# The second layer's context in one run of matmuls instead of two halves, with its pointwise work moved to other slots

## The chip, the cores and the metric

The kernel runs on one core of one Trainium2 chip. The metric is the time on the device in microseconds (us), the median of several executions. Engines are named as the profile names them: PE is TensorE, DVE is VectorE, ACT is ScalarE, POOL is GpSimd, SP is SyncE with the DMA queue.

## The reference, cut to what matters

128 samples of 64 tokens with 768 features go through a two-layer graph attention, all in float32, and `x` is added at the end:

```python
h = jnp.maximum(_layernorm(x, axis=-1), 0.0)
for l in range(2):
    ...                                   # attention from h, W_left, W_right, adj
    h_lin = jnp.einsum('bsh,oh->bso', h, W_lin[l]) + b_lin[l]
    ctx = jnp.matmul(attention, h_lin)    # 64x64 by 64x768 for each sample
    h = relu(_layer_norm(ctx, ln_a[l], ln_b[l]))
return x + h
```

The last pass of the kernel computes the last three lines of layer 1, for 16 blocks (0 to 15) of 8 samples. A block is four tiles of 128 tokens by 768.

## The kernel before

TensorE forms `h_lin` of a block from 15 products (0 to 14) of sums of token columns with sums of weights. Each product goes to one of the PSUM banks X, Y, Z, V, and ScalarE or VectorE adds the bank into `hl`. Two products that use the same bank wait for each other: product 10 writes the bank X that product 8 has left, so it needs VectorE's two reads of product 8. GpSimd forms the 11 token sums `ts` of the next block from `ht`, after ScalarE has applied the affine (`Relu(scale * ht + bias)`) to it.

The context of block `u - 1` is computed between the products of block `u`. In the second layer it comes in two halves, behind products 0 and 7, and its pointwise work is put at numbered slots, two a product (slot 2i after the first half of product i, slot 2i+1 after its read). A slot sets only the place in each engine's queue.

```python
def scaled(k):                                     # in finish(u, r): one half
    if last:
        nc.vector.scalar_tensor_tensor(zs[k], cx[k], rs[:, k:k + 1], rows["a"], op0=ALU.mult, op1=ALU.mult)
        nc.gpsimd.tensor_add(zs[k], zs[k], rows["b"])          # the bias sum
        return
    ...
def done(k):
    if last:
        xs = XS[u, r]                              # the residual sum: max with 0, plus x
        nc.vector.scalar_tensor_tensor(xs[k], zs[k], 0.0, xs[k], op0=ALU.max, op1=ALU.add)
        ...                                        # store, then load the next x
...
put_all(9 if u else 15, affine(2, l, u + 1))             # ScalarE: one of six a slot
put_sums_t((2, l, u + 1), 15 if u else 21, 1, 0)         # GpSimd: the 11 sums
ends = {}
if u and last:
    ends = {0: ((u - 1, 0), (6, 7, 8, 11, 12)), 7: ((u - 1, 1), (20, 21, 22, 30, 30))}
elif u > NB - 3:
    ends = {5: ((u - 1, 0), (16, 17, 18)), 11: ((u - 1, 1), (28, 29, 30))}
elif u:
    ends = {12: (u - 1, None)}                     # layer 0: the whole context behind product 12
```

The five slot numbers of a half are those of the inverse deviation, two scalings and two residual sums. (Reshapes are cut from the code.)

Of the kernel before, what the change touches and what calls it, by code (L numbers as in the profile page):

```python
# [10 lines left out]
F32 = mybir.dt.float32  # L11
I32 = mybir.dt.int32
AF = mybir.ActivationFunctionType
ALU = mybir.AluOpType
# [3 lines left out]
def kernel(  # L18
# [24 lines left out]
    nc = tc.nc  # L43
    B, S, H = x.shape
# [32 lines left out]
    def put(slot, *fs):  # L77
        plan.setdefault(slot, []).extend(fs)

    def put_all(slot, fs, step=1):  # L80
        for f in fs:
            if f is not None:
                put(slot, f)
            slot += step
        return slot
# [537 lines left out]
    def pass_two(l, aside):  # L623
        last = l == L - 1
        with tc.tile_pool(name=f"two{l}", bufs=2, reuse_waits="tile") as sp:
# [48 lines left out]
            def batch(r, k, h):  # L674
                return 4 * (h if k == 0 else 1 - h) + r + 2 * k
# [46 lines left out]
            def residual(u, r):  # L722
                XS[u, r] = [sp.tile([P, H], F32, name="xr", bufs=4) for _ in range(2)]
                for k in range(2):
                    for h in range(PAIR):
                        nc.sync.dma_start(XS[u, r][k][h * S:(h + 1) * S], x[u * NBB + batch(r, k, h)])  # L726

            def finish_block(u, more):

                parts = context_block(u)  # L730
                tiles = ((0, 0), (0, 1), (1, 0), (1, 1))
                zs = {t: sp.tile([P, H], F32, name="z", bufs=4) for t in tiles}
                cut = (slice(0, T), slice(T, H))

                for t in ((1, 1), (1, 0)):
                    nc.vector.tensor_copy(zs[t][:, cut[0]], parts[t][0])
                    parts[t][0] = zs[t][:, cut[0]]
                    if t == (1, 1):
                        AHEAD.append(fresh(l, 0, more))
                ss = stat.tile([P, Q, 2], F32, name="ssb", bufs=2)  # L740
                sd = stat.tile([P, Q], F32, name="sdb", bufs=2)
                rs = stat.tile([P, Q], F32, name="rsb", bufs=2)

                def squares(t):
                    junk = zs[0, t[1]]
                    for n in range(2):
                        nc.scalar.activation(junk[:, cut[n]], parts[t][n], AF.Square,
                                             accum_out=ss[:, 2 * t[0] + t[1], n:n + 1])

                def deviation():  # L750
                    nc.vector.reduce_sum(sd, ss, axis=mybir.AxisListType.X)
                    nc.scalar.activation(sd, sd, AF.Sqrt, bias=floor, scale=1.0 / (H - 1.0))

                def inverse():
                    nc.vector.tensor_scalar_add(rs, sd, EPS_LN)
                    nc.vector.reciprocal(rs, rs)

                def scaled(t):
                    by = rs[:, 2 * t[0] + t[1]:2 * t[0] + t[1] + 1]
                    for n in range(2):  # L760
                        nc.scalar.activation(zs[t][:, cut[n]], parts[t][n], AF.Copy, scale=by)
                    kept(u, *t, zs[t])

                order = ((1, 1), (1, 0), (0, 0), (0, 1))
                for f, slots in ((squares, (25, 26, 28, 29)), (scaled, (33, 34, 35, 36))):
                    for n, t in zip(slots, order):
                        put(n, lambda f=f, t=t: f(t))
                put(30, deviation)
                put(32, inverse)

            def kept(u, r, k, z):
                for h in range(PAIR):
                    nc.sync.dma_start(ROWS[u][batch(r, k, h)], z[h * S:(h + 1) * S])

            def finish(u, r):

                cx = context(u, r)
                zs = [sp.tile([P, H], F32, name="z", bufs=4) for _ in range(2)]
                if last and not u and not r:
                    residual(u, r)  # L780
                two = "p (n d) -> p n d"
                ss = stat.tile([P, 2], F32, name="ss", bufs=2)
                sd = stat.tile([P, 2], F32, name="sd1", bufs=2)
                rs = stat.tile([P, 2], F32, name="rs1", bufs=2)
                for k in range(2):
                    nc.scalar.activation(zs[k].rearrange(two, n=2), cx[k], AF.Square, accum_out=ss[:, k:k + 1])

                nc.scalar.activation(sd, ss, AF.Sqrt, bias=floor, scale=1.0 / (H - 1.0))

                def inverse():  # L790
                    nc.vector.tensor_scalar_add(rs, sd, EPS_LN)
                    nc.vector.reciprocal(rs, rs)

                def scaled(k):
                    if last:
                        nc.vector.scalar_tensor_tensor(  # L796
                            zs[k].rearrange(two, n=2), cx[k], rs[:, k:k + 1],
                            rows["a"].rearrange(two, n=2), op0=ALU.mult, op1=ALU.mult)
                        nc.gpsimd.tensor_add(zs[k], zs[k], rows["b"])  # L799
                        return  # L800
                    if (u, r, k) == (NB - 1, 1, 1):
                        nc.vector.tensor_scalar_mul(zs[k].rearrange(two, n=2), cx[k], rs[:, k:k + 1])
                    else:
                        nc.scalar.activation(zs[k].rearrange(two, n=2), cx[k], AF.Copy, scale=rs[:, k:k + 1])
                    kept(u, r, k, zs[k])

                def done(k):
                    if last:
                        xs = XS[u, r]
                        nc.vector.scalar_tensor_tensor(xs[k], zs[k], 0.0, xs[k], op0=ALU.max, op1=ALU.add)  # L810
                        for h in range(PAIR):
                            nc.sync.dma_start(out[u * NBB + batch(r, k, h)], xs[k][h * S:(h + 1) * S])
                        if k and u + r < NB - 1:
                            residual(u + r, 1 - r)

                steps = [lambda f=f, k=k: f(k) for f in (scaled, done) for k in range(2)]
                return [inverse] + (steps if last else steps[:2])

# [36 lines left out]
            for u in range(NB):  # L855
                turn = not last and u >= NB - 2
                put(4, lambda u=u: load_at(u))
                if u + 1 < NB:
                    load_h(2, l, u + 1)
                    put_all(9 if u else 15, affine(2, l, u + 1))  # L860
                    put_sums_t((2, l, u + 1), 15 if u else 21, 1, 0)
                    if turn:
                        load_rows(1, 0, sp)
                        put_all(10, transpose_rows(1, 0, sp), 2)
                    if u in aside:
                        aside[u]()
                    ends = {}
                    if u and last:
                        ends = {0: ((u - 1, 0), (6, 7, 8, 11, 12)), 7: ((u - 1, 1), (20, 21, 22, 30, 30))}
                    elif u > NB - 3:  # L870
                        ends = {5: ((u - 1, 0), (16, 17, 18)), 11: ((u - 1, 1), (28, 29, 30))}
                    elif u:
                        ends = {12: (u - 1, None)}
                    linear(u, (0, 1), 0, ends, (0, 1) if u + 2 < NB else (0,))
                    for n in sorted(plan):
                        plan[n - 30] = plan.pop(n)
                else:
                    if turn:
                        load_h(1, 1, 0)
                        put_all(28, affine(1, 1, 0), 3)  # L880
                        put_sums_t((1, 1, 0), 38, 2, 30)
                        ends = ({1: ((u - 1, 0), (13, 14, 16)), 11: ((u - 1, 1), (34, 35, 36))},
                                {4: ((u, 0), (50, 51, 52))})
                    else:
                        last_block(u)
                        ends = ({0: ((u - 1, 0), (12, 13, 15, 22, 24)), 9: ((u - 1, 1), (28, 29, 30, 39, 41))},
                                {2: ((u, 0), (44, 48, 51, 61, 62))})
                    linear(u, (0,), 0, ends[0], (1,))
                    linear(u, (1,), 30, ends[1], ())
                    for n in sorted(plan):  # L890
                        run(n)
                    for f in (finish_last if last else finish)(u, 1):
                        f()
# [48 lines left out]
```

## Time and profile before

| | us |
|---|---|
| time, median of 3 | 2758.04 (2754.77 to 2759.26) |
| span of the profiled run | 2756.7 |
| TensorE busy | 2726.2 |
| one steady block of the last pass | 29.20 |
| one block of the first layer, context in one run | 28.84 |

The view of busy time by stretch, for one steady block of the last pass. The columns are the stretch and its length, then the busy time of PE, PEld, DVE, ACT and POOL with their instruction counts, then the granted TensorE clock (1.00 is full speed), the DMA share and GB/s.

```profile
core 0: us, PE busy (x) PEld busy (x) DVE busy (x) ACT busy (x) POOL busy (x), PEclk, DMA share, GB/s
2392.16:2421.36 29.20, 29.20 (x156) 23.59 (x152) 19.89 (x25) 13.63 (x26) 23.64 (x16) 1.00 0.59 167
```

TensorE has not a gap in 29.20 us. VectorE (19.89) and GpSimd (23.64) both have idle time, but a residual sum of VectorE can't be placed anywhere in it: the 60 of the last pass (128x768) take 946 ns at best and 2023 in the median, and two took 4.00 us at 2401.78, while GpSimd worked throughout.

### The profile page before, as it was taken

Reading aid. Unit: us, or ns where it says so; the run is one execution under the profiler, and the core shown is the slowest. Engines: PE = TensorE matmul, PEld = TensorE weight load, DVE = VectorE, ACT = ScalarE, POOL = GpSimd, SP = SyncE. Lnnn points to the kernel's source line nnn. Section 1 sums busy time; section 2 is a strip of 40 time slices with the busy share of each in tenths; the row PEclk is TensorE's granted clock in tenths of the full one; section 3 lists DMA queues with packets and bytes.
Section 4 is the critical chain, followed back from the end, with each engine's and each line's share of the span. In section 5 each row is a group of like instructions: output and inputs, shape, how many; then the busy total and the mean of one; then the engine's idle time right before and its main releaser. Section 6 shows DMA issues by size and latency. Waiting matters only on the chain. (4 is left out here: it accounts for less than half of the span.)

```text
span 2756.7 us, 46373 instructions
## 1 busy us (share of the span) xinstructions
PE 2726.2 (99%) x18712; PEld 2339.2 (85%) x18712; DVE 1347.4 (49%) x2269; ACT 849.5 (31%) x1611; POOL 1192.3 (43%) x935
## 2 busy tenths in 40 slices
PE   8999999999999999999999999999999999999998
PEld 7888888888888888888788888888888887888886
DVE  6455445545454333333335444544444335676666
ACT  3222223222321154444621211121122214444443
POOL 3432352224223555655522443223222325887885
PEclk9999999999999999999999999999999999999999
DMA  6534433343332333343555333443344204555655
GB/s 196 128 75 98 121 81 81 90 120 90 76 80 72 102 109 117 116 155 124 149 126 151 94 75 78 116 112 75 76 101 120 57 26 145 164 168 164 178 161 143
DMA packets 234072, 310.82 MB, mean 113 GB/s; under 512 B 54146, under 2 KB 184450, under 8 KB 225666
## 3 DMA queue, kind: packets, MB, share of 16 engines
q1 hardware_dynamic: 233698, 307.45, 41.6%
q8 instruction: 149, 2.44, 0.4%
q14 instruction: 65, 0.53, 0.1%
q10 hardware_dynamic: 160, 0.39, 0.0%
HBM read 202.91 MB, written 104.86 MB: 112 GB/s over the span
## 5 line engine op out<-in xcount | busy, mean ns | idle before, releaser
L155 POOL TENSOR_TENSOR ts<-ht 128x512 f32<-128x512 f32 x441 | 586.7, 1340 | 1223.8 <-DMA ht<-h 523.1
L203 ACT ACTIVATE m<-X 128x512 f32<-128x512 f32 (+1 forms) x256 | 151.5, 592 | 1086.0 <-PE X L429 570.1
L155 POOL TENSOR_TENSOR ts<-ht,ts 128x512 f32<-128x512 f32 x189 | 248.8, 1323 | 135.4 <-PE X L833 60.6
L155 DVE TENSOR_TENSOR m<-m,V 128x512 f32<-128x512 f32 (+1 forms) x256 | 173.3, 677 | 270.0 <-PE V L429 269.8
L155 DVE TENSOR_TENSOR m<-m,X 128x512 f32<-128x512 f32 (+1 forms) x256 | 162.9, 677 | 249.8 <-PE X L429 249.1
L833 PE MATMUL X<-w_n,ts 128*128 128x256 f32 x1024 | 244.3, 380 | 2.5 <-ACT X L619 1.7
L429 PE MATMUL X<-ts,w_l 128*128 128x256 f32 x1024 | 242.7, 380 | 0.1
L429 PE MATMUL X<-ts,w_r 128*128 128x252 f32 (+1 forms) x1024 | 238.7, 376 | 0.0
L155 DVE TENSOR_TENSOR m<-m,Z 128x512 f32<-128x512 f32 (+1 forms) x128 | 87.5, 683 | 306.0 <-ACT m L203 246.1
L833 PEld LDWEIGHTS X<-w_n,ts 128*128 128x128 f32 x1024 | 191.5, 190 | 35.0 <-issue 3.1
L429 PEld LDWEIGHTS X<-ts,w_l 128*128 128x128 f32 x1024 | 192.0, 190 | 30.2 <-DVE m L155 2.7
L429 PEld LDWEIGHTS X<-ts,w_r 128*128 128x128 f32 x1024 | 192.0, 190 | 26.0
L275 ACT ACTIVATE ht<-ht,b_col,a_col 128x512 f32<-128x512 f32 x192 | 143.6, 804 | 151.3 <-DMA ht<-h 151.3
L833 PE MATMUL Y<-w_n,ts 128*128 128x256 f32 x768 | 182.5, 379 | 0.0
L429 PE MATMUL Y<-ts,w_l 128*128 128x256 f32 x768 | 181.5, 379 | 0.4 <-DVE w_l L155 0.4
L429 PE MATMUL Y<-ts,w_r 128*128 128x252 f32 (+1 forms) x768 | 179.2, 376 | 1.3 <-POOL w_r L155 1.3
L429 PEld LDWEIGHTS Y<-ts,w_l 128*128 128x128 f32 x768 | 145.8, 190 | 20.6 <-DVE w_l L155 0.8
L833 PEld LDWEIGHTS Y<-w_n,ts 128*128 128x128 f32 x768 | 145.8, 190 | 20.4 <-issue 0.6
L429 PEld LDWEIGHTS Y<-ts,w_r 128*128 128x128 f32 x768 | 145.8, 190 | 19.1 <-POOL w_r L155 1.7
L155 DVE TENSOR_TENSOR hl<-hl,V 128x512 f32<-128x512 f32 (+1 forms) x136 | 89.0, 655 | 129.4 <-PE V L833 112.1
L203 ACT ACTIVATE hl<-X 128x512 f32<-128x512 f32 (+1 forms) x135 | 77.9, 577 | 222.2 <-PE X L833 219.3
L799 POOL TENSOR_TENSOR z<-z,b 128x768 f32<-128x768 f32 x62 | 111.9, 1816 | 79.4 <-DVE z L796 79.4
(163 smaller groups left out, 4729.5 us busy)
## 6 DMA issues: line engine op xcount, KB each, us to landing
ht<-h SPq DMA_DIRECT2D x63, 1536.0 KB, 7.2
h<-xb SPq DMA_DIRECT2D x124, 384.0 KB, 5.9
z<-z SPq DMA_DIRECT2D x128, 192.0 KB, 3.1
x<-z SPq DMA_DIRECT2D x128, 192.0 KB, 8.5
x<-in_x_dram SPq DMA_DIRECT2D x120, 192.0 KB, 8.4
xr<-in_x_dram SPq DMA_DIRECT2D x120, 192.0 KB, 3.8
out_dram<-xr SPq DMA_DIRECT2D x120, 192.0 KB, 2.7
adj<-in_adj_dram SPq DMA_DIRECT2D x64, 128.0 KB, 2.7
```

The source lines that it names most:

```text
L155: (eng.tensor_add if sign == "+" else eng.tensor_sub)(o, a, b)
L203: nc.scalar.activation(to(o), p, AF.Copy, scale=1.0 if sign == "+" else -1.0)
L275: nc.scalar.activation(ht, ht, AF.Relu, bias=cols[1][:, c:c + 1], scale=cols[0][:, c:c + 1])
L429: nc.tensor.matmul(p[:, g], w[ORDER[i][0]][:, c, g * P:(g + 1) * P], b()[t][:, c, :].rearrange(bs, s=S)[:, :, :ns], start=(new and g == c ...
L799: nc.gpsimd.tensor_add(zs[k], zs[k], rows["b"])
L833: nc.tensor.matmul(p[:, n], b[t][:, c, r * P:(r + 1) * P], w[s][:, c, :], start=(i in FIRST and i not in PRELOAD and n == c == 0), stop=(c ...
```

## The change

Its intent: the last pass does as the first layer does, so that TensorE changes between its 128x128 and its 64x64 tiling once a block instead of twice. In blocks 1 to 10 the context of the block before stands in one run behind product 12; the four residual sums stand in a row behind the read of product 5, "where GpSimd rests". The last five blocks step back to halves, each a little earlier, since the end needs them early. In block 12 the affines and GpSimd's sums stand four slots later (`late`).

```diff
 def finish_block(u, more):                # the whole context of a block
-        nc.vector.tensor_copy(zs[t][:, cut[0]], parts[t][0])
+        (nc.scalar.copy if last else nc.vector.tensor_copy)(zs[t][:, cut[0]], parts[t][0])
 ...
+                        if last:
+                            nc.vector.scalar_tensor_tensor(to, parts[t][n], by, rows["a"][:, cut[n]],
+                                                           op0=ALU.mult, op1=ALU.mult)
 ...
+                    if last:
+                        nc.gpsimd.tensor_add(zs[t], zs[t], rows["b"])
 ...
+                put_each(squares, (26, 27, 28, 29) if last else (25, 26, 28, 29))
+                put_each(scaled, (29, 30, 33, 34) if last else (33, 34, 35, 36))
+                if last:
+                    put_each(lambda t: added_to(u, *t, zs[t]), (41, 42, 43, 44))   # slots 11 to 14 of the next block
 ...
-                    put_all(9 if u else 15, affine(2, l, u + 1))
-                    put_sums_t((2, l, u + 1), 15 if u else 21, 1, 0)
+                    late = 4 if last and u == NB - 4 else 0
+                    put_all(late + (9 if u else 15), affine(2, l, u + 1))
+                    put_sums_t((2, l, u + 1), late + (15 if u else 21), 1, 0)
 ...
-                    if u and last:
-                        ends = {0: ((u - 1, 0), (6, 7, 8, 11, 12)), 7: ((u - 1, 1), (20, 21, 22, 30, 30))}
+                    ends = {12: (u - 1, None)} if u else {}
+                    if last and u > NB - 6:       # blocks 11, 12, 13, 14; NB is 16
+                        ends = ({8: ((u - 1, 0), (22, 23, 24, 31, 33)), 13: ((u - 1, 1), (32, 33, 34, 39, 41))},
+                                {5: ((u - 1, 0), (16, 17, 18, 30, 32)), 11: ((u - 1, 1), (28, 29, 30, 36, 38))},
+                                {3: ((u - 1, 0), (12, 13, 14, 15, 16)), 9: ((u - 1, 1), (24, 25, 26, 32, 33))},
+                                {1: ((u - 1, 0), (8, 9, 10, 13, 14)), 7: ((u - 1, 1), (20, 21, 22, 30, 30))})[u - NB + 5]
+                    if last and u:
+                        residuals(u - 1, ...)     # loads of x at slots of their own
```

Left out: the split of the deviation into two pairs of tiles, and the same rearrangement in block 15.

More of the change, by code (lines that the diff above doesn't have):

```diff
@@ L726, in residual, with residuals @@
                         nc.sync.dma_start(XS[u, r][k][h * S:(h + 1) * S], x[u * NBB + batch(r, k, h)])
+            def residuals(u, slots):
+                for r, slot in sorted(enumerate(slots), key=lambda s: s[1]):
+                    put(slot, lambda r=r: residual(u, r))
             def finish_block(u, more):
                 parts = context_block(u)
-                tiles = ((0, 0), (0, 1), (1, 0), (1, 1))
-                zs = {t: sp.tile([P, H], F32, name="z", bufs=4) for t in tiles}
+                order = ((1, 1), (1, 0), (0, 0), (0, 1))
+                zs = {t: sp.tile([P, H], F32, name="z", bufs=4) for t in order}
                 cut = (slice(0, T), slice(T, H))
-                for t in ((1, 1), (1, 0)):
-                    nc.vector.tensor_copy(zs[t][:, cut[0]], parts[t][0])
+                for t in order[:2]:
+                    (nc.scalar.copy if last else nc.vector.tensor_copy)(zs[t][:, cut[0]], parts[t][0])
                     parts[t][0] = zs[t][:, cut[0]]
@@ L748, in squares, with deviation, inverse @@
                                              accum_out=ss[:, 2 * t[0] + t[1], n:n + 1])
-                def deviation():
-                    nc.vector.reduce_sum(sd, ss, axis=mybir.AxisListType.X)
-                    nc.scalar.activation(sd, sd, AF.Sqrt, bias=floor, scale=1.0 / (H - 1.0))
-                def inverse():
-                    nc.vector.tensor_scalar_add(rs, sd, EPS_LN)
-                    nc.vector.reciprocal(rs, rs)
+                def deviation(q):
+                    nc.vector.reduce_sum(sd[:, q], ss[:, q], axis=mybir.AxisListType.X)
+                    nc.scalar.activation(sd[:, q], sd[:, q], AF.Sqrt, bias=floor, scale=1.0 / (H - 1.0))
+                def inverse(q):
+                    nc.vector.tensor_scalar_add(rs[:, q], sd[:, q], EPS_LN)
+                    nc.vector.reciprocal(rs[:, q], rs[:, q])
                 def scaled(t):
@@ L760, in scaled, with put_each, added_to @@
                     for n in range(2):
-                        nc.scalar.activation(zs[t][:, cut[n]], parts[t][n], AF.Copy, scale=by)
-                    kept(u, *t, zs[t])
-                order = ((1, 1), (1, 0), (0, 0), (0, 1))
-                for f, slots in ((squares, (25, 26, 28, 29)), (scaled, (33, 34, 35, 36))):
-                    for n, t in zip(slots, order):
-                        put(n, lambda f=f, t=t: f(t))
-                put(30, deviation)
-                put(32, inverse)
+                        to = zs[t][:, cut[n]]
+                        if last:
+                            nc.vector.scalar_tensor_tensor(to, parts[t][n], by, rows["a"][:, cut[n]],
+                                                           op0=ALU.mult, op1=ALU.mult)
+                        else:
+                            nc.scalar.activation(to, parts[t][n], AF.Copy, scale=by)
+                    if last:
+                        nc.gpsimd.tensor_add(zs[t], zs[t], rows["b"])
+                    else:
+                        kept(u, *t, zs[t])
+                def put_each(f, slots):
+                    for n, t in zip(slots, order):
+                        put(n, lambda t=t: f(t))
+                put_each(squares, (26, 27, 28, 29) if last else (25, 26, 28, 29))
+                for q, n, m in ((slice(2, 4), 27, 29), (slice(0, 2), 30, 32)) if last else ((slice(0, 4), 30, 32),):
+                    put(n, lambda q=q: deviation(q))
+                    put(m, lambda q=q: inverse(q))
+                put_each(scaled, (29, 30, 33, 34) if last else (33, 34, 35, 36))
+                if last:
+                    put_each(lambda t: added_to(u, *t, zs[t]), (41, 42, 43, 44))
+            def added_to(u, r, k, z):
+                xs = XS[u, r][k]
+                nc.vector.scalar_tensor_tensor(xs, z, 0.0, xs, op0=ALU.max, op1=ALU.add)
+                for h in range(PAIR):
+                    nc.sync.dma_start(out[u * NBB + batch(r, k, h)], xs[h * S:(h + 1) * S])
             def kept(u, r, k, z):
@@ L778, in finish @@
                 zs = [sp.tile([P, H], F32, name="z", bufs=4) for _ in range(2)]
-                if last and not u and not r:
-                    residual(u, r)
                 two = "p (n d) -> p n d"
@@ L807, in done @@
                 def done(k):
-                    if last:
-                        xs = XS[u, r]
-                        nc.vector.scalar_tensor_tensor(xs[k], zs[k], 0.0, xs[k], op0=ALU.max, op1=ALU.add)
-                        for h in range(PAIR):
-                            nc.sync.dma_start(out[u * NBB + batch(r, k, h)], xs[k][h * S:(h + 1) * S])
-                        if k and u + r < NB - 1:
-                            residual(u + r, 1 - r)
+                    added_to(u, r, k, zs[k])
                 steps = [lambda f=f, k=k: f(k) for f in (scaled, done) for k in range(2)]
@@ L866, in pass_two @@
                         aside[u]()
-                    ends = {}
-                    if u and last:
-                        ends = {0: ((u - 1, 0), (6, 7, 8, 11, 12)), 7: ((u - 1, 1), (20, 21, 22, 30, 30))}
-                    elif u > NB - 3:
+                    ends = {12: (u - 1, None)} if u else {}
+                    if not last and u > NB - 3:
                         ends = {5: ((u - 1, 0), (16, 17, 18)), 11: ((u - 1, 1), (28, 29, 30))}
-                    elif u:
-                        ends = {12: (u - 1, None)}
+                    if last and u > NB - 6:
[4 more added lines that the diff above has]
+                    if last and u:
+                        residuals(u - 1, ((16, 20), (8, 16), (6, 13), (1, 8))[u - NB + 5] if u > NB - 6 else (20, 18))
                     linear(u, (0, 1), 0, ends, (0, 1) if u + 2 < NB else (0,))
@@ L885, in pass_two @@
                         last_block(u)
+                        residuals(u - 1, (0, 8))
                         ends = ({0: ((u - 1, 0), (12, 13, 15, 22, 24)), 9: ((u - 1, 1), (28, 29, 30, 39, 41))},
```

## The prediction

> **What bounds the kernel now.** I read the busy totals first, then the list of who waited for whom for TensorE alone, cut to the last pass (from 2300 us, the second layer's h_lin, context and output), then TensorE's timeline of one block in each layer.
>
> ```profile
> PE 2726.2 (99%) x18712; PEld 2339.2 (85%) x18712; DVE 1347.4 (49%) x2269; ACT 849.5 (31%) x1611; POOL 1192.3 (43%) x935
> ```
>
> ```profile
> PE V L833 <- DVE hl L155: 2.1, 1, 2.1
> PE X L833 <- ACT X L619: 1.7, 1, 1.7
> ```
>
> TensorE is the bound: 99% busy, and in the 455 us of the last pass it waits twice, 1.7 us at the entry and 2.1 us in the last block. Time can come only out of what TensorE does itself. The first layer already forms its context in one run, so the two layers can be laid side by side. First layer (rows: start, duration, engine, line, operation):
>
> ```profile
> 1022.29 1.99 PE L833 MATMUL Z<-w_n,ts 128*128 128x256 f32 x8
> ...
> 1046.57 1.89 PE L833 MATMUL V<-w_n,ts 128*128 128x256 f32 x8
> 1048.38 0.65 PE L671 MATMUL Y<-hl,at 64*64 64x512 f32 x2
> ...
> 1049.29 1.90 PE L671 MATMUL aux<-hl,at 64*64 64x256 f32 x24
> 1051.13 1.13 PE L833 MATMUL Z<-w_n,ts 128*128 128x256 f32 x4
> ```
>
> Second layer, the same block work with the context in two halves:
>
> ```profile
> 2392.16 1.99 PE L833 MATMUL Z<-w_n,ts 128*128 128x256 f32 x8
> ...
> 2402.63 1.89 PE L833 MATMUL Y<-w_n,ts 128*128 128x256 f32 x8
> 2404.45 1.52 PE L648 MATMUL aux<-hl,at 64*64 64x384 f32 x16
> 2405.90 1.99 PE L833 MATMUL X<-w_n,ht 128*128 128x256 f32 x8
> 2407.73 1.89 PE L833 MATMUL V<-w_n,ht 128*128 128x256 f32 x8
> ...
> 2421.36 1.99 PE L833 MATMUL Z<-w_n,ts 128*128 128x256 f32 x8
> ```
>
> The reader is to see the two periods: 1051.13 - 1022.29 = 28.84 us against 2421.36 - 2392.16 = 29.20 us. A product in the stream takes 1.727 us. Around a half it is 2407.73 - 2402.63 = 5.10 us for two products and the half, so a half costs 5.10 - 3.45 = 1.65 us and two cost 3.29. The one run costs 2.94 by the same subtraction (1.81 + 2.75 + 1.83 - 3.45). Difference 0.35 to 0.36.
>
> The third reading is what DVE and GpSimd do to each other. The last pass's residual sum (max with 0, plus x; line 810) reads two SBUF tiles:
>
> ```profile
> L810 DVE SCALAR_TENSOR_TENSOR xr<-z,xr x60: 946/2023/2561, 2314.9 to 2736.9; 128x768 f32<-128x768 f32 x60
> ```
>
> ```profile
> 2401.17 0.69 DVE L155 TENSOR_TENSOR hl<-hl,V 128x512 f32<-128x512 f32 x1 [0.91 <-PE V L833]
> 2401.78 4.00 DVE L810 SCALAR_TENSOR_TENSOR xr<-z,xr 128x768 f32<-128x768 f32 x2
> 2408.00 1.28 DVE L155 TENSOR_TENSOR hl<-hl,X 128x512 f32<-128x512 f32 x2 [2.23 <-PE X L833]
> ```
>
> ```profile
> 2399.42 3.60 POOL L799 TENSOR_TENSOR z<-z,b 128x768 f32<-128x768 f32 x2 [3.78 <-DVE z L796]
> 2402.98 3.93 POOL L155 TENSOR_TENSOR ts<-ht 128x512 f32<-128x512 f32 x2
> ```
>
> A residual sum takes 946 ns at best and 2023 in the median. In this stretch GpSimd never rests: two sums take 4.00 us, and GpSimd's own two, 1.27 us each when alone, take 3.93.
>
> [...] around each 64x64 stretch the neighbours slip by about 0.09 us on entry and 0.10 on return[...]. One run instead of two saves one such set. [...] 4.00 us is two DVE turns of 0.8 to 0.9 and two GpSimd waits. The scaling (line 796), with one input in PSUM, stays at 1005 to 1018 ns whatever GpSimd does.
>
> **The change, part by part.**
> 1. TensorE. In blocks 1 to 10 of the last pass the context of the block before moves into one run after the 13th product. Columns and number of matmuls are the same (8 of 512 and 8 of 256 against 16 of 384). Ten blocks x 0.36 us = -3.6 us. Blocks 11 to 15 keep halves, only at other products: 0.
> 2. ACT. It gains two copies out of the X and Y banks (0.5 us apart in its queue) and has eight squares instead of four (0.98 us of queue per tile with accumulator reads, as in the first layer), and a second Sqrt. It is 31% busy; only its queue order matters. Block-relative (B = start of product 0, period 28.84): copies from B-5.2, first two tiles until B-1.7, Sqrt at B-0.7, the others until B+1.4, second Sqrt after DVE's small sum at about B+2.5, so the read of product 0 ends at about B+3.35. Product 2 writes that bank again from B+3.45. Just in time: 0 to 0.15 us a block, call it 1 us in all.
> 3. DVE scaling: from PSUM or z, two pieces for a tile, 1.1 us instead of 1.0. It lies at B+1.2 to B+7.2 where DVE is free.
> 4. GpSimd. Bias sums of four tiles together, B+3.1 to B+10.3 (4 x 1.8). The next block's 11 sums (1.27 each) cannot start before the first four of ACT's affines of its tokens are done: in the trace above affines end 3.4 us after ACT takes product 4's read, which puts the first sum at B+12.35. They end near B+28.
> 5. DVE residual sums: four in a row behind the read of product 5, from B+11.2. DVE must be back at B+15.8 for the two reads of product 8, since product 10 (B+17.27) adds to the same bank and the first layer's margin there is only 0.18 us. Undisturbed, four x 0.87 end at B+14.7: free. But my count lets the first GpSimd sum ask at B+12.35, during the second residual sum; then two GpSimd turns come between, the third and fourth take 2.0 each, DVE is back at B+17.0, and product 10 waits about 1.0 us. If the GpSimd sum asks 0.6 us later, it waits behind the third instead, the last ends at B+15.9, and nothing is lost.
> 6. Loads of x go from behind the output stores to fixed slots; 0. The 1.7 us wait at the entry is in block 0, untouched. The 2.1 us wait in the last block comes from a residual sum of 2.23 us caught by GpSimd's sum of line 696; the last block's slots are unchanged, so it stays, within 1 us.
>
> Sum without the stall of part 5: 2758.04 - 3.6 + 1 = 2755.4. With it in all ten blocks: + 10 = 2765.
>
> **The rivals.** (a) Gain of 0.36 a block and no new wait, 2754.5 to 2755.5. For it: the last pass of the kernel before has no wait in its steady blocks, so its slots were placed with the lock in view, and the change's own words put the residual sums where GpSimd rests. (b) A wait takes the place of the saving: TensorE waits for DVE before the 11th product, 0.5 to 1.1 us a block, 2760 to 2766. For it: the count of part 5; against it: it hangs on 0.6 us in GpSimd's start. (c) The copies on ACT make TensorE wait for ACT at the third product, up to 0.5 us a block: 2758 to 2760. If DVE's scaling from z meets GpSimd's lock there, this is likelier; GpSimd should be done with its sums by then. (d) The blocks 11 to 14, whose halves stand close together (products 8 and 13), lose a microsecond or two through the two PSUM tiles of the context not being read in time; the scaling of the first half ends about 0.5 us before the second half needs them.
>
> **Range and chances.** I give (a) about 0.6, (b) and (c) together 0.4. The middle of that mixture lies a little above (a): 2756 us, 0.07% down. The range 2752 to 2766 holds (a) with the usual spread of the runs (2754.77 to 2759.26 for the kernel before) and (b) in full. Two per cent is 55 us. No part here can move that: the whole of the context costs 16 x 3.3 = 53 us. So within 2% is all but certain.
>
> **What would show it.** Right: the one-run blocks of the last pass repeat every 28.84 us on TensorE; TensorE's waits there name no engine beyond the two known ones; residual sums at about 0.95 us in most of them. Rival (b): a row in TensorE's waits X <- DVE hl, ten times about 1 us, periods near 29.9, and residual sums in pairs of 0.95 and 2.0. Rival (c): X <- ACT hl at the third product. The prediction is wrong outside its range if GpSimd's sums slip into the next block, so that products wait for their tokens, or if a wait on the store of an output holds up the load of the next block's tokens in the SP queue, which I place at B+23 with landing near 8 us later, seven before ACT needs them.

The sum came to 2755.4 us without the stall and to 2765 with it, as it stands above.

## The result, and the profile after

The changed kernel took 2769.94 us (median of 4 runs, 2769.54 to 2770.78), the kernel before in the same rounds 2757.78 (4 runs). The ratio is 1.0046, 95% interval 1.0028 to 1.0063: the same at the 2% mark, but 12 us slower and 4 us above the predicted range. Ratios here are the mean time of one kernel's runs over that of the other's in the same rounds, so not quite the ratio of the quoted medians. The profiled span is 2768.4 us.

TensorE's waits in the last pass of the changed kernel (bank and line, releaser, total us, times, longest):

```profile
PE X L852 <- DVE hl L155: 10.2, 10, 3.4
PE V L852 <- DVE hl L155: 2.4, 1, 2.4
PE Y L852 <- DVE hl L155: 0.7, 1, 0.7
PE X L852 <- ACT X L619: 0.6, 1, 0.6
```

The first row is new. Nine of its ten waits are 0.75 to 0.76 us, in blocks 2 to 10; the tenth is 3.4 us and stands in block 13. The same stretch view as above, for block 6, shows the wait as idle time of TensorE: 29.85 us long and 29.10 busy.

```profile
2449.30:2479.15 29.85, 29.10 (x153) 23.68 (x152) 19.47 (x30) 15.12 (x38) 23.22 (x15) 1.00 0.56 165
```

The timeline of block 6 around that wait (start, duration, engine, line, operation; in brackets the idle time before and its releaser):

```profile
2459.91 0.69 DVE L155 TENSOR_TENSOR hl<-hl,V 128x512 f32<-128x512 f32 x1 [2.36 <-issue]
2460.52 5.71 DVE L794 SCALAR_TENSOR_TENSOR xr<-z,xr 128x768 f32<-128x768 f32 x4
...
2461.62 3.79 POOL L155 TENSOR_TENSOR ts<-ht 128x512 f32<-128x512 f32 x2 [2.04 <-PE X L852]
...
2464.84 1.89 PE L852 MATMUL V<-w_n,ht 128*128 128x256 f32 x8
...
2466.15 1.27 DVE L155 TENSOR_TENSOR hl<-hl,X 128x512 f32<-128x512 f32 x2
...
2467.48 1.99 PE L852 MATMUL X<-w_n,ts 128*128 128x256 f32 x8 [0.75 <-DVE hl L155]
2469.31 1.89 PE L852 MATMUL Y<-w_n,ts 128*128 128x256 f32 x8
```

Read it from the bottom. Product 10 (2467.48) waits for VectorE's reads of product 8, which start at 2466.15, when four residual sums have ended that took 5.71 us. GpSimd's first sum asked at 2461.62, during the second of them. The block starts at 2449.30, so that is B+12.3. The view counts 0.75 us as idle because it gives product 9 a length of 1.89 us; by starts, product 10 is 0.91 us late (2464.84 + 1.727 against 2467.48) and then needs 1.83 instead of 1.73 us to product 11. Together that is 1.02 us, the difference between the period of 29.86 and the 28.84 that was predicted without a stall.

Starts of product 0, block by block, account for the last pass. From the start of block 1 to that of the second half of block 15 the kernel before takes 427.60 us, the changed kernel 439.78:

| part | us |
|---|---|
| blocks 1 to 10, one run instead of two halves: 10 x (28.84 - 29.20) | -3.6 |
| stall at product 10: block 2 (30.04 - 28.84) and blocks 3 to 10 (8 x 1.02) | +9.4 |
| blocks 11, 12 and 14: 29.19, 29.20, 29.19 | 0 |
| block 13: 35.29 against 29.20 | +6.1 |
| block 15: the known wait is 2.4 instead of 2.1 us | +0.3 |
| sum | +12.2 |

All that stands before block 1 came 0.5 us earlier in this run. The start of block 1 varies from 2298.9 to 2303.3 us over the profiles here, kernels of both kinds, so I read blocks and not totals.

Block 13 of the changed kernel, from the timeline:

```profile
2647.61 3.59 POOL L824 TENSOR_TENSOR z<-z,b 128x768 f32<-128x768 f32 x2 [9.38 <-DVE z L821]
...
2666.39 3.60 POOL L824 TENSOR_TENSOR z<-z,b 128x768 f32<-128x768 f32 x2
...
2668.24 2.56 DVE L794 SCALAR_TENSOR_TENSOR xr<-z,xr 128x768 f32<-128x768 f32 x1 [6.02 <-POOL z L824]
...
2676.28 4.32 DVE L794 SCALAR_TENSOR_TENSOR xr<-z,xr 128x768 f32<-128x768 f32 x2 [1.16 <-DMA xr<-in_x_dram]
...
2681.86 2.59 PE L852 MATMUL X<-w_n,ts 128*128 128x256 f32 x8 [3.44 <-DVE hl L155]
2684.24 3.03 PE L852 MATMUL Y<-w_n,ts 128*128 128x256 f32 x8
```

In block 12 the sums stand four slots later, and GpSimd idles 9.38 us before a bias sum. It then carries the 11 sums 9 us into block 13 (2666.39 - 2656.99), the bias sums of the context come behind them, and the residual sum that needs them holds VectorE's queue for 6.02 us. The later residual sums then stand late in front of the reads of product 8, and product 10 waits 3.44 us. There is a second loss in the last two rows: the two products take 2.38 and 2.86 us from start to start instead of 1.73. The stretch view gives the reason, in the column of the granted clock:

```profile
2683.12:2686.53 3.41, 3.41 (x10) 2.71 (x9) 1.28 (x2) 0.59 (x1) 3.33 (x3) 0.50 0.94 323
```

The clock is 0.50 for 3.41 us, so 1.71 us of work is lost. Waits of 3.44 and 0.65 us, 1.71 us at half clock and some 0.1 us for each restart make up the 6.1 us.

### The profile page after: what moved, and what is told of

Its sections match the earlier page's. It is cut to its first block, busy times and chain, and to the rows that moved or that the text cites. A ratio compares the mean times of both kernels' runs of the same rounds, so it can differ in the third digit from the quotient of the medians.

```text
span 2768.4 us, 46493 instructions
## 1 busy us (share of the span) xinstructions
PE 2728.3 (99%) x18712; PEld 2341.1 (85%) x18712; DVE 1341.1 (48%) x2329; ACT 865.2 (31%) x1711; POOL 1183.6 (43%) x935
## 5 line engine op out<-in xcount | busy, mean ns | idle before, releaser
L155 POOL TENSOR_TENSOR ts<-ht 128x512 f32<-128x512 f32 x441 | 575.2, 1315 | 1242.1 <-DMA ht<-h 561.1
L155 POOL TENSOR_TENSOR ts<-ht,ts 128x512 f32<-128x512 f32 x189 | 240.2, 1278 | 135.6 <-PE X L852 60.5
L852 PEld LDWEIGHTS X<-w_n,ts 128*128 128x128 f32 x1024 | 190.7, 190 | 49.2 <-DVE hl L155 15.9
L155 DVE TENSOR_TENSOR hl<-hl,X 128x512 f32<-128x512 f32 (+1 forms) x136 | 83.0, 651 | 120.9 <-PE X L852 116.8
L456 PEld LDWEIGHTS aux<-m,ht 128*32 128x32 f32 x6144 | 126.4, 110 | 13.5 <-issue 13.2
```

The lines of the kernel that those rows point to most:

```text
L155: (eng.tensor_add if sign == "+" else eng.tensor_sub)(o, a, b)
L456: nc.tensor.matmul(p[h * S + e:h * S + e + 32, q, e:e + 95], ht[:, c, b * S + e:b * S + e + 32], mb[:, e:e + 95], start=(c == 0), stop=(c ...
L852: nc.tensor.matmul(p[:, n], b[t][:, c, r * P:(r + 1) * P], w[s][:, c, :], start=(i in FIRST and i not in PRELOAD and n == c == 0), stop=(c ...
```

## The experiments

Theory: VectorE's residual sums and GpSimd's token sums take turns ("the lock" in the texts below), and that holds the reads of product 8 (stall of 1.02 us); block 13 is lost to `late = 4`. The rival for the first is that VectorE or its order is at fault without GpSimd; the rival for the second is that block 13's own slots are at fault. Each timed run was compared with the kernel before on the same chip (medians 2757.12, 2758.03 and 2759.21 us).

**e1_psum_operand.** The residual sums of blocks 2 to 11 read their second operand from PSUM. Its output is wrong, which doesn't matter for the time.

```diff
-    nc.vector.scalar_tensor_tensor(xs, z, 0.0, xs, op0=ALU.max, op1=ALU.add)
+    nc.vector.scalar_tensor_tensor(xs, z, 0.0, other, op0=ALU.max, op1=ALU.add)   # other: the context's PSUM tile
```

> The changed kernel, with the four residual sums of the one-run blocks taking their second operand from PSUM in place of the x tile in SBUF (wrong results on purpose; same slots, same size, same loads and stores). Lock theory (DVE with two SBUF inputs is blocked by GpSimd): the four sums take about 1.0 us each, 4.0 together in place of 5.7, the wait of TensorE for DVE before the 11th product vanishes in blocks 2 to 10, their period falls from 29.86 to 28.84 us, and the time from 2769.9 by 9 x 1.02 = 9.2 to about 2760.7. Rival (four sums are simply too many for the gap between product 5's and product 8's reads, lock or not): the wait stays, 2769 to 2770.

Measured: 2761.59 us, ratio 1.0016 (1.0001 to 1.0031). Block 2 takes 29.03 us, blocks 3 to 10 28.84, block 13 still 35.3. VectorE's row in the timeline of block 6:

```profile
2458.94 3.54 DVE L794 SCALAR_TENSOR_TENSOR xr<-z,aux 128x768 f32<-128x768 f32 x4
```

Same instructions, same order, same slots: 3.54 us instead of 5.71, and the stall is gone. GpSimd was busy from 2460.04 us on, from the second of the four to the end, and did not hold them, with one of their operands in PSUM.

**e2_affine_one_later.** The affines and the sums of the next tokens one slot later in blocks 2 to 10; the result is right.

```diff
-late = 4 if last and u == NB - 4 else 0
+late = 4 if last and u == NB - 4 else 1 if last and 1 < u < NB - 5 else 0
```

> The changed kernel, with ACT's affines of the next block's tokens one slot later in blocks 2 to 10, so that the fourth affine falls behind the read of product 6 and GpSimd's first sum asks at about 14.2 us after the block's start in place of 12.3. Lock theory, with the threshold of 0.6 us that the prediction named: all four residual sums run undisturbed (3.7 us together), no wait before product 10, period 28.84, about 2760.7 us. Rival (DVE's own load): unchanged 2769.9. Second rival (GpSimd's sums then slip past the block's end and meet the scaling of the next): period between 28.9 and 29.8 with a wait for ACT at the third product.

Measured: 2760.15 us, ratio 1.0014 (0.9997 to 1.0031); blocks 3 to 10 28.84 us. The timeline of block 6:

```profile
2454.82 3.56 DVE L794 SCALAR_TENSOR_TENSOR xr<-z,xr 128x768 f32<-128x768 f32 x4
...
2457.79 2.96 POOL L155 TENSOR_TENSOR ts<-ht 128x512 f32<-128x512 f32 x2 [3.90 <-ACT ht L275]
```

GpSimd now asks 2.97 us after the first residual sum begins, during the fourth; no residual sum waits, and GpSimd waits once. The stall hung on one slot in another engine's queue. Block 13 took 36.44 us here, with 6.8 us at half clock instead of 3.4.

**e3_block12_not_late.** The changed kernel with `late` 0 everywhere.

```diff
-late = 4 if last and u == NB - 4 else 0
+late = 0
```

> The changed kernel without the delay of four slots in block 12. Theory: that delay lets GpSimd idle 9.4 us in block 12 and finish its sums 9 us into block 13, where its bias sum then comes late, DVE waits 6.0 us for it, and TensorE waits 0.65 + 3.44 and more; block 13 has 35.29 us in place of 29.20. Without it block 13 falls to 29.2 to 30, the time by about 6 to 2764. Rival (the halves at products 3 and 9 of block 13, or the late loads of x, cost it whatever block 12 does): block 13 stays above 33 us, time above 2768; or block 12 takes a new wait of 1 to 3 us from the lock and part of the gain is lost.

Measured: 2767.02 us, ratio 1.0033 (1.0018 to 1.0048). Block 13 takes 30.7 us instead of 35.29, block 12 29.81 instead of 29.20. So `late = 4` costs 4.6 us in block 13 and saves 0.6 in block 12, where ScalarE's read of product 6 otherwise comes late behind two affines. The rival as written (block 13 above 33 us, or a wait of 1 to 3 us from the lock in block 12) did not come, but 1.5 us of block 13 stay. The time fell by 2.9 us and not by the 6 expected: besides the 1.5 and the 0.6, the profile has 3.41 us at half clock in the last block (1.7 us lost), which the changed kernel did not have there.

**e4_both.** The edits of e2 and e3 together.

```diff
+late = 1 if last and 1 < u < NB - 5 else 0
```

> Both of the two last edits together. If the two losses are separate and add up: 2769.9 - 9.2 - 6 = about 2754.7, 3 us under the kernel before, which is what ten blocks at 0.36 us each give. If they are tied to each other: above 2757.

Measured: 2757.06 us, ratio 0.9999 (0.9984 to 1.0014), where I had expected less. The blocks add up as they should: 28.92, 29.03, eight times 28.84, 29.2, 29.81, 30.69, 29.19. TensorE's longer waits in its last pass:

```profile
PE V L852 <- DVE hl L155: 2.1, 1, 2.1
PE X L852 <- DVE hl L155: 1.4, 1, 1.4
```

The 1.4 us are in block 13. What the two rows do not hold is the third loss. The stretch view just behind the 2.1 us wait, first of this kernel, then of the next (e5), which has the same wait:

```profile
2727.42:2730.84 3.42, 3.42 (x9) 2.68 (x9) 2.27 (x3) 0.66 (x2) 1.63 (x1) 0.50 0.99 332
```

```profile
2723.70:2727.12 3.42, 3.42 (x21) 2.45 (x24) 2.60 (x4) 1.62 (x5) 1.68 (x1) 1.00 1.01 320
```

The counts (x9, x21) do not compare, since the second stretch holds 13 matmuls of products and 8 of a 64x64 context half. By starts, a matmul of a product takes 0.43 us in the first stretch and 0.215 in the second: half clock. The last section comes back to the waits before it.

**e5_block13_sums_later.** e4, with the two residual sums of block 13's first half behind the reads of product 8.

```diff
-{3: ((u - 1, 0), (12, 13, 14, 15, 16)), ...
+{3: ((u - 1, 0), (12, 13, 14, 18, 20)), ...
```

> As e4_both, with one more edit: in block 13 of the last pass the two residual sums of the first half move from the slots just before the reads of product 8 to slots just after them and after the read of product 9. Theory: in e4_both product 10 of block 13 waits 1.4 us because the two residual sums stand ahead of those reads on VectorE, begin late (1.0 us for GpSimd's bias sums) and take 4.49 us against 1.9 alone, in turns with GpSimd's sums. Moved behind the reads they are just as slow but nobody waits: block 13 goes from 30.69 to about 29.3 us, TensorE's wait X <- DVE hl of 1.4 us goes, total 1.4 us under e4_both. Rival: VectorE is simply full there, and the wait moves to the reads of product 10, so that block 13 stays above 30.3.

Measured: 2754.16 us, ratio 0.9993 (0.998 to 1.0007). Block 13 takes 29.19 us and its wait is gone. My theory said that the two sums would be as slow as before, only in nobody's way; they took 1.34 and 1.43 us instead of 4.49 together. The rest of block 13's loss was thus in its own slots.

**e6_gpsimd_sums_moved.** e4, with GpSimd's two sums for the x of the last block at other slots.

```diff
-zip(XS[u, 1], (26, 45))
+zip(XS[u, 1], (33, 43))
```

> As e4_both, with one more edit: the two sums of GpSimd that add the bias to the x of the last block move from slots 26 and 45 to 33 and 43, where VectorE does no residual sum. Theory: the 2.1 us wait (V <- DVE hl) that every kernel here has in the last block comes from one residual sum of 2.23 us held by the first of these sums; it becomes about 0.95 us and the wait falls to about 0.8 us or less, a gain of 1.3 us. The granted clock showed 0.50 for about 3.3 us right behind this wait in the profiles of three of the six kernels so far, which costs 1.65 us more; if the wait sets it off, a shorter wait leaves it out and this run keeps 1.00 there. Rival: the wait is not for the residual sum but for VectorE's whole queue, and stays above 1.5 us.

Measured: 2755.75 us, ratio 0.999 (0.9975 to 1.0005). The wait of 2.1 us falls to 0.81 as expected, but a new one of 0.91 us appears (X <- DVE hl) a few products later. The clock stayed at 1.00 in the last block.

**e7_three_repairs.** e4 with the edits of e5 and e6, and in block 12 four of the six affines before the squares of the context half.

```diff
+if last and u == NB - 4:
+    for f, n in zip(affine(2, l, u + 1), (8, 9, 10, 10, 13, 14)):
+        put(n, f)
```

> e4_both with both edits of the two runs before, and in block 12 ScalarE does four of its six affines before the squares of the context half rather than two before and two behind, so that its read of product 6 is not late. Theory: block 12 goes from 29.81 to 29.2, block 13 from 30.69 to about 29.3, the last wait from 2.1 to 0.8; all together about 3.3 us under e4_both and under the kernel before, 2753.5 to 2754.5. Rival: GpSimd's sums now ask about 4 us earlier in block 12 and hold VectorE's residual sums there, so that block 12 or 13 loses 1 us again.

Measured: 2753.43 us, ratio 0.9987 (0.9974 to 0.9999). Blocks 11 to 14 take 29.2 us each, so the rival for block 12 falls. The new wait of e6 is here too. GpSimd's timeline in the last block shows its cause:

```profile
2724.64 3.58 POOL L824 TENSOR_TENSOR z<-z,b 128x768 f32<-128x768 f32 x2 [6.49 <-DVE z L821]
2728.20 4.29 POOL L696 TENSOR_TENSOR ht<-ht,b 128x768 f32<-128x768 f32 x2
```

The two moved sums (line 696) run at once behind the bias sums, though one has a slot ten later than the other. Its operands are there and nothing else stands before it in GpSimd's queue. They fall on two residual sums of VectorE, which take 2.16 and 2.23 us.

**e8_affine_one_earlier.** e4 with `late = -1` in blocks 2 to 10: a dose of the lock.

```diff
-late = 1 if last and 1 < u < NB - 5 else 0
+late = -1 if last and 1 < u < NB - 5 else 0
```

> As e4_both, but in blocks 2 to 10 the affines and GpSimd's sums of the next tokens stand one slot earlier than in the changed kernel (two earlier than in e4_both). Dose of the lock: GpSimd's first sum asks about 0.86 us earlier, during the first residual sum instead of the second, so three of the four residual sums go in turns with GpSimd: the group takes about 6.7 us instead of 5.71, VectorE is back about 1 us later, product 10 waits about 2.0 us and the period is about 30.8 us. Rival: the number of turns does not follow from when GpSimd asks; the period stays at 29.86.

Measured, one run of unknown state: 2775.34 us, with periods of 30.93 us in blocks 3 to 10 (expected: about 30.8). Timeline:

```profile
2464.58 6.78 DVE L794 SCALAR_TENSOR_TENSOR xr<-z,xr 128x768 f32<-128x768 f32 x4
...
2464.98 3.63 POOL L155 TENSOR_TENSOR ts<-ht 128x512 f32<-128x512 f32 x2 [1.34 <-ACT ht L275]
```

GpSimd asks 0.40 us after the first residual sum begins, so during the first (B+11.62, 0.70 us earlier than in the changed kernel; 0.86 was expected): three of the four wait a turn. With 3.56 us for none held (e2), 5.71 for two and 6.78 for three, a held residual sum costs 1.07 to 1.08 us more.

**e9_second_sum_last and e10_last_block_too.** e7 with the second of GpSimd's two sums between the last two bias sums; then also block 14's second residual sum behind two reads in the last block.

```diff
-zip(XS[u, 1], (33, 43))
+zip(XS[u, 1], (33, 49))
 # e10 besides:
-ends = ({0: ((u - 1, 0), (12, 13, 15, 22, 24)), ...
+ends = ({0: ((u - 1, 0), (12, 13, 15, 22, 27)), ...
```

> As e7_three_repairs, but GpSimd's second sum for the x of the last block stands between the last two bias sums of GpSimd. In e7 both sums ran back to back (4.29 us), straight behind the two bias sums, because a slot sets only the order in GpSimd's queue and not the time, and they held the two residual sums of the last block (2.16 and 2.23 us): a new wait of 0.91 us (X <- DVE hl). Theory: with one of the two sums gone from there the second residual sum takes 0.95 us and this wait goes; the last residual sums are at most 0.5 us later, so 0.4 to 0.9 us under e7. Rival: the sum in its new place holds the last residual sums on the path to the end, and the total is as in e7 or above.

> As e9_second_sum_last, and the second residual sum of block 14's first half moves behind the reads of products 12 and 13 of the last block's first run. Theory: the wait of 0.81 us that is left there (V <- DVE hl) is for reads that stand behind this residual sum of 0.95 us on VectorE; it goes to 0 or 0.1, so 0.7 to 0.8 us under e9 and 2752 or below, 0.2 per cent under the kernel before. Rival: the bank is then read in time but the next thing in the queue (the scaling for the first context half) comes 0.9 us late, and the saving is lost at the end.

Measured: e9 2752.72 us, ratio 0.9978 (0.9965 to 0.999); e10 2752.05 us, ratio 0.9976 (0.9962 to 0.999). In e9 the wait of 0.91 us goes, but from the second half of block 15 to the end it takes 28.9 us, in e7 28.7 and in e5 27.8: the gain is given back after the last product, as its rival said. e10 takes TensorE's last wait: in its profile TensorE waits for nothing from 2300 us on, block 15's first half takes 16.62 instead of 17.49 us, and 0.3 of that comes back in the second half (29.2). In e9 and e10 the last two residual sums take 2.93 us instead of e7's 1.82: GpSimd's last bias sum, which the moved sum has pushed back, holds the first of them.

e10 is the fastest here, 0.2% under the kernel before and about 0.7% under the changed one (0.9976 over 1.0046). In its profile the last pass explains -4.2 us against the kernel before (422.1 instead of 427.6 up to the second half of block 15, and 1.3 more behind that). The rest of the 7 us between the medians is outside what I edited: what stands before block 1 was 2.2 us shorter in that run.

## Why the prediction was wrong

Two steps failed. Part 1 put 0 on blocks 11 to 15, where block 13 lost 6.1 us; and the weights put a stall-free block first, where product 10 stalled in nine blocks and cost 9.4 us.

*Part 1, the saving.* Right where it was worked out: 28.84 us a block in e1, e2 and e4, 0.36 under 29.20. The slips at entry and return explain 0.19 of it (0.09 + 0.10); most of the rest is inside the stretches, since two halves take 2 x 1.45 us by starts and the one run 2.75 for the same columns. No run shows why. Part 1 was wrong in its last sentence, "Blocks 11 to 15 keep halves, only at other products: 0." This term was worth +6.1 us, all in block 13. Without it the result would be about 2763.8 us, inside the range in spite of the stall. I had looked at where the halves stand and not at what `late = 4` in block 12 does to GpSimd's queue in block 13. Rival (d) did expect a loss in blocks 11 to 14, but of a microsecond or two and through the context's PSUM tiles. The runs showed 4.6 us from `late = 4` (e3) and 1.5 from two residual sums ahead of the reads of product 8 (e5). Part of the 6.1 was no wait at all but half clock.

*Part 2, ScalarE.* Right in kind: 1 us was allowed. The repaired kernels lose 0.07 us in block 1 and 0.19 in block 2 and nothing later. Rival (c) did not happen.

*Part 3, the scaling.* No wait comes from it.

*Parts 4 and 5, the lock.* The count was right. The first sum asked at B+12.3 (predicted 12.35), two residual sums were held, VectorE was back at B+16.85 (predicted 17.0), and product 10 cost 1.02 us (predicted 1.0). The residual sums took 0.95, 0.95, 2.03 and 2.02 us, as rival (b) said they would. "0.6 us later and nothing is lost" was not tested: e2 asks 1.87 us later (B+14.19) and loses nothing. By the count, one held sum would end at B+15.85 (11.22 + 3.56 + 1.07), near the 15.9 predicted. The failing step here is the weight. I gave 0.6 to (a), on the argument that the slots had been placed with the lock in view, and took 2756 as the estimate, against my own count, which said 2765. The stall was there in nine blocks, not ten, since block 1 takes 28.91 us.

*Part 6, the loads.* 0 in the steady blocks. In block 13 one wait of 1.16 us names a load of x, but there the queue was already late: the load stands in the SP queue behind the store of the residual sum that had waited 6.02 us. The wait at the entry was 0.6 us instead of 1.7; it lies before block 1, in the stretch that varies from profile to profile.

With the sums put right: -3.6 + 9.4 + 6.1 + 0.3 = +12.2 us. The chances for within 2% were right.

## What to carry to other kernels

Where two engines hold each other, as here (1.07 to 1.08 us for each held residual sum), "this engine rests here" is true only until its next operand arrives: look up when the other engine asks and count the turns, and believe the count over the intention of whoever placed it. When a change delays one engine's queue on purpose, follow that queue into the next stage and see who stands behind it. A wait of TensorE can cost more than its length (the 3.44 us in block 13 were followed by 3.41 us at half clock, 1.71 us more), so read the granted clock in stretches of a few microseconds behind every wait.

## What the traces show of the half clock and of the turns

- *Half clock behind a wait.* In block 13 the wait of 3.44 us in the changed kernel and that of 3.46 us in e1 were each followed by 3.41 us at a granted clock of 0.50; in e2, with a wait of 3.45 us, it was 6.83 us (2669.98 to 2676.81), of which the first 1.08 us lie inside the wait. In the last block the waits of 2.09 us in e1, 2.39 in e3 and 2.1 in e4 were each followed by 3.4 us at 0.50. Behind 2.39 us in the changed kernel, 2.10 in the kernel before, 2.09 in e5 and 2.22 in e2 the clock stayed at 1.00. So the length of a wait does not tell these apart: at 2.39 us e3 lost 1.7 us more and the changed kernel nothing. Apart from e2's, the stretches begin 0.7 to 1.3 us behind the end of the wait. What decides was not shown: each kernel has one profiled execution, and no run was made for it.
- *Turns of VectorE and GpSimd.* Four residual sums with both operands in SBUF take 3.56 us with none held (e2), 5.71 with two (the changed kernel) and 6.78 with three (e8), so each held one costs 1.07 to 1.08 us more; with one operand in PSUM the four take 3.54 us (e1). A small instruction can be held too: in the changed kernel VectorE's addition to 128x2 deviations took 1.23 us at 2630.30, while GpSimd did two token sums (2628.29 to 2631.50), and 0.17 us at 2641.85, while GpSimd did nothing.
